# A second token group's linear attention started beside the first, in borrowed tiles, with new due times

## The chip, the cores and the metric

The kernel runs on one core of a Trainium2 chip. The core has five engines with one instruction queue each: TensorE (PE in the profile; its weight loads are PEld) multiplies matrices, VectorE (DVE), ScalarE (ACT) and GpSimd (POOL) work elementwise, and SyncE (SP) here issues every DMA. Each engine executes its own instructions in the order in which they were issued and waits for the other engines by semaphores. The metric is the time of one execution on the device in microseconds (us); lower is better.

## The reference, cut to what matters

The input is 8 sequences of 1024 tokens of width 256, all in float32. Four layers are applied one after the other, each to a layernorm of the running sum `x`:

```python
x = x + _L0_attn_ref(_layernorm(x), ...)   # linear ("flow") attention, then Wo, norm, a 256-1024-256 GELU block, norm
x = x + _L0_ffn_ref(_layernorm(x), ...)    # a 256-1024-256 ReLU block
x = x + _L1_attn_ref(_layernorm(x), ...)   # softmax attention over the whole sequence
x = x + _L1_ffn_ref(_layernorm(x), ...)    # gated block of width 704, inputs and weights rounded to 4-bit values
```

The linear attention of the first layer is where the change is. For one sequence, with `q` and `k` behind a sigmoid:

```python
sink_in = normal / einsum('bhld,bhld->bhl', q + EPS, cumsum(k, axis=2) + EPS)
src_out = normal / einsum('bhld,bhld->bhl', k + EPS, cumsum(q, axis=2) + EPS)
cons_sink = einsum('bhld,bhld->bhl', q + EPS, cumsum(k * src_out[..., None], axis=2) + EPS) / normal
cons_src  = einsum('bhld,bhld->bhl', k + EPS, cumsum(q * sink_in[..., None], axis=2) + EPS) / normal
...
kv = cumsum(einsum('bhld,bhlm->bhldm', k, vs), axis=2)
x  = einsum('bhld,bhldm->bhlm', qs, kv) * sink_alloc[..., None]
```

All the running sums go along the tokens of one sequence, from its first token to its last.

## The kernel before, in words

**Tiles and groups.** Tokens are taken in chunks of 128 (`P`), and chunks in groups of four (`G = 4`, 512 tokens). A sequence has `NCH = 8` chunks and so `NG = 2` groups; the eight sequences have `flows = 16` groups. `divmod(p, NG)` gives the sequence and the half of it that group `p` is: groups 0 and 1 are the first and the second half of the first sequence.

**Stages.** `linear_group(p)` (L998) does the linear attention of one group. Its inner `front(i)` (L1008) takes the chunk `x` that a DMA has loaded, normalizes it, turns it into the columns of `n0T` by `flip` and asks for the chunk four further on. `linear_span` (L1051) then projects `q` and `k` (512 columns a matmul, 256 in group 0, which is cut into two spans), takes the four running sums on VectorE (`running`, L943, which starts from the carry of the group before unless the group opens a sequence), multiplies and sums them by head on TensorE (`head_sums`, L886), and turns the packed results `r1`, `flow`, `e`, `div`, `scale` and `comp` into scales. `spread` (L901) brings packed rows back to full width by way of DRAM, with two `packed` stores and four or two `spread` loads of 256 KB on the SP queue; group 0 does it with small mask matmuls instead (`spread_near`, L922). `linear_chunk` (L1213) does values, scores, the running `kv` and the output projection, chunk by chunk; chunk `c` has its turn when `count["v"] == c`. Its last step hands the normalized `h` over to the dense stage.

`dense` (L1435) runs the two blocks of width 1024. Their weights don't stay: `load_weights` (L1480) streams them again for every group, two buffers of 256 KB for `w_in` and two for `w_out` (`W_FF = 2`). `norms_1` and `norms_2` do what lies between and behind; `norms_2` writes `n2T`, a tile with four buffers, for the softmax layer. `soft_chunk` (L1603) does softmax attention and the 4-bit block for one chunk, and starts for a sequence when both groups of it have passed `norms_2`. Its wide rows lie in three `hid` tiles. `fp4_weights` rounds the weights of the last block once (tiles `w_raw`), `softmax_weights` prepares `wqk` once (tiles `wqk_raw`).

**What sets the order.** No order is written out. All these are generators that a planner, `Plan` (L76), resumes while the program is built. Each `yield` names an engine, the tiles it needs, perhaps a condition (`when`) and a due time (`at`), in units of a group: group `p`'s steps are due at `p` plus a constant from the table `T` (L31). The planner keeps its own clocks of the engines, tiles and DMA rings from costs in `took` (L176). In `run` (L330) it resumes the part with the least key: first how long TensorE would wait, then by how much the part misses a margin of readiness (`RIPE`, from `ripe_t` for TensorE, `ripe_v` for VectorE and so on), then the due time. So every constant of `T` can move instructions anywhere. Two decisions of the planner add work. Where it sees TensorE pause for more than 1.6 us, `fill` (L1757) puts matmuls of the identity with itself there. And `flip` (L683) turns a tile on TensorE when `idle` (L315) finds too little ready for it, or else by a POOL copy (`cut`), a DMA transpose (`spun`) and an ACT copy.

**Order around the change.** `linear_attention` (L1423) runs `linear_group(p)` for `p = 0 ... 15`, one after the other. A group begins when all values of the groups before it are done (`count["v"] == p * G`, L1028), and its projections when the output projections before it are done (`count["linear"] >= p * G`, L1076). It needs `n0T`, `q` and `k`, which have one buffer each (L1029, L1034).

Of the kernel before, what the change touches and what calls it, by code (L numbers as in the profile page):

```python
# [9 lines left out]
F32 = mybir.dt.float32  # L10
# [7 lines left out]
P = 128  # L18
# [6 lines left out]
V_PADS = 2  # L25
HB = P // 2
SCW = P + HB
W_FF = 2
RES = 10
HALVES = 5  # L30
T = dict(  # L31
    span=-0.073, prods=0.117, pair=0.137, sums=0.05, weighted=0.269, sums2=0.303, chunk=0.625,
    scores=0.819, turn_k=0.822, xo=0.419, turn_h=0.629, step=0.095, dense=-0.049, norm=0.528,
    soft=3.5, soft1=0.277, soft2=0.575, soft3=0.75, fp4=3.15, fp4_over=4.022, tail=11,
    weights=0.069, shy=0.745, ripe_t=0.935, ripe_v=0.744, ripe_s=0.298, ripe_g=0.0, ripe_d=6.94,
    back=0.51, ahead=1.173, stage=3, lin=0.0,
)
LAG = 2
QB = 16
G = 4  # L40
GT = G * P
# [34 lines left out]
class Plan:  # L76
# [206 lines left out]
    def pe(self, *tiles, **kw):  # L283
        return self.need("tensor", tiles, **kw)

    def dve(self, *tiles, **kw):
        return self.need("vector", tiles, **kw)
# [4 lines left out]
    def dma(self, *tiles, **kw):  # L292
        return self.need("sync", tiles, **kw)
# [101 lines left out]
def block_stack_kernel(ctx: ExitStack, tc: tile.TileContext, a: dict, out: bass.AP):  # L395
# [20 lines left out]
    plan = Plan(tc, tc.nc)  # L416
    nc, pe, dve, act, dma = plan, plan.pe, plan.dve, plan.act, plan.dma
# [6 lines left out]
    big = ctx.enter_context(tc.tile_pool(name="big", bufs=1))  # L424
# [33 lines left out]
    def kept(shape, name, bufs):  # L458
        t = big.tile(shape, F32, tag=name, name=name, bufs=bufs)
        return t  # L460

    def small(shape, name, bufs=4):
        t = sm.tile(shape, F32, tag=name, name=name, bufs=bufs)
        return t
# [39 lines left out]
    for e in range(2):  # L504
        h = slice(e * HB, (e + 1) * HB)
# [32 lines left out]
    hids = [const.tile([P, INTER_PAD], F32, name=f"hid{i}") for i in range(TILES["hid"][0])]  # L538
# [74 lines left out]
    xs = {c: load_x(c) for c in range(2)}  # L613
# [123 lines left out]
    def two(t):  # L737
        return t.rearrange("p (k t) -> p k t", k=2)
# [144 lines left out]
    weights = set()  # L883
# [59 lines left out]
    def running(out, cur, carry, b, first, last):  # L943
# [14 lines left out]
    flows = B * NG  # L958
    seqs = [{"past": {"chunks": 0}, "n2T": {}, "vt": {}, "normed": 0} for _ in range(B)]
    groups = [  # L960
        {"res": {}, "hT": {}, "nT": {}, "turned": {}, "scaled": set(), "ran": set()}
        for _ in range(flows)
    ]
    count = {
        "halves": 0,
        "dense": 0,
        "acc": 0,
        "res": 0,
        "v": 0,
        "scored": 0,  # L970
        "attended": 0,
        "linear": 0,
# [25 lines left out]
    def linear_group(p):  # L998
        s, g = divmod(p, NG)
        past = seqs[s]["past"]  # L1000
        first, last = g == 0, g == NG - 1
        if first:
            past["cur"] = small([P, 4], "carry_cur", 2)
            past["w"] = small([P, 4], "carry_w", 2)

        n0T = None

        def front(i):  # L1008
            c = p * G + i
            x = xs.pop(c)  # L1010
            yield dve(x, when=lambda: count["res"] < RES)
            count["res"] += 1
            rc = groups[p]["res"][i] = kept([P, D], "res", RES)
            n0 = yield from layernorm("n0", x)
            plan.drop(x)
            yield from flip(two(n0), n0T[:, :, i * P : (i + 1) * P], near=p == 0)
            fronts.add(i)
            yield plan.need("gpsimd", (n0, bo), when=lambda: "norm" in late)
            nc.gpsimd.tensor_tensor(rc, n0, bo, ALU.add)
            plan.drop(n0)  # L1020
            if c + G < B * NCH:
                need = dma(when=lambda: count["stage"] >= 2)
                need.fresh = "x"
                yield need
                xs[c + G] = load_x(c + G)

        fronts = set()
        yield dve(at=p + T["lin"], when=lambda: count["v"] == p * G)  # L1028
        n0T = two(kept([P, 2 * GT], "n0T", 1))  # L1029
        for i in range(G):  # L1030
            plan.start(front(i), p + T["lin"] + 0.5 * T["step"] * i - (p == 0 and i < 2))
        tiles = SimpleNamespace(
            n0T=n0T,
            qk=[kept([P, 2, GT], name, 1) for name in ("q", "k")],  # L1034
            total=small([P, 1], "total", 2),
            ahead=small([P, 1], "ahead", 2),
            comp=small([P, G, 32], "comp", 1),
            packed={n: small([P, P], n, 1) for n in ("r1", "flow", "e", "div", "scale")},
        )
        if first:  # L1040
            past["before"] = None
        else:
            past["before"] = past["total"]
        past["total"] = tiles.total

        spans = (range(0, 2), range(2, 4)) if p == 0 else (range(G),)
        for span in spans[1:]:
            plan.start(linear_span(p, span, fronts, tiles), p + 0.01)
        yield from linear_span(p, spans[0], fronts, tiles)

    def linear_span(p, span, fronts, tiles):  # L1051
# [3 lines left out]
        first, last = g == 0, g == NG - 1  # L1055
        opens, closes = first and span.start == 0, last and span.stop == G
        ran = groups[p]["ran"]
# [3 lines left out]
        r1, flow, e, div, scale = (  # L1061
            tiles.packed[n][rows] for n in ("r1", "flow", "e", "div", "scale")
        )
        n0T, qk = tiles.n0T, tiles.qk
# [2 lines left out]

        def turn(n):

            return lambda: span.start == 0 or (n, span.start) in ran  # L1070


        yield pe(
            at=p + T["lin"] + T["span"] + after,
            when=lambda: fronts >= set(span)
            and count["linear"] >= p * G  # L1076
            and turn("flows")(),
        )
        cur = [qk[b // 2][:, b % 2, here] for b in range(4)]
        for b in (2, 0, 3, 1):  # L1080
# [18 lines left out]
        prods = [None] * 4  # L1099
        for n, pair in enumerate(((2, 0), (3, 1))):  # L1100
            for b in pair:
                need = dve(cur[b], at=p + T["lin"] + T["prods"] + T["pair"] * n + after, when=turn("flow"))
# [15 lines left out]
        if near:  # L1118
            weighted = yield from spread_near(flow, span, ((2, 0), (3, 1)))
        else:  # L1120
            weighted = yield from spread(flow, (2, 0, 3, 1))
        count["stage"] = max(count["stage"], 2)

        for n, pair in enumerate(((2, 0), (3, 1))):
            for b in pair:
                w = weighted[b]
                need = dve(w, at=p + T["lin"] + T["weighted"] + T["pair"] * n + after, when=turn("scale"))
# [40 lines left out]
        ahead = tiles.ahead[rows]  # L1168
# [36 lines left out]
        comp = tiles.comp  # L1205
# [215 lines left out]
        yield from turn_half(p, "hT", i, h)  # L1421

    def linear_attention():  # L1423
        for p in range(flows):
            yield from linear_group(p)
        yield pe(when=lambda: count["linear"] == B * NCH)
        plan.spare = True
        for n in ("q", "k"):
            h = kept([P, 2, GT], n, 1).rearrange("p k t -> p (k t)")
            nc.gpsimd.memset(h[:, INTER:INTER_PAD], 0.0)  # L1430
            hids.append(h[:, :INTER_PAD])
        plan.size["hid"] += 2


    def dense():  # L1435
# [44 lines left out]
        def load_weights(names, used, loaded, first):  # L1480

            ws, n = [], 0
            for p in range(flows):
                for name in names:
                    for f in 2 * list(range(0, NF, 2)):
                        yield dma(
                            at=p + 0.9 + T["weights"] + (2 * n % 32 + (0 if first else LAG)) / 32,
                            when=lambda: n < W_FF + used[0] // 2 and count["stage"] >= 2,
                            unused=ws[n - W_FF :][:1] if n >= W_FF else (),
                        )  # L1490
                        tag = "w_in" if first else "w_out"
                        w = big.tile([P, 2, 2 * P], F32, tag=tag, name=tag, bufs=W_FF)
                        if first:
                            src_ = a[name][:, f * P : (f + 2) * P].rearrange("(k p) n -> p k n", p=P)
                            views = [w[:, :, j * P : (j + 1) * P] for j in range(2)]
                        else:
                            src_ = a[name][f * P : (f + 2) * P, :].rearrange("(j p) n -> p j n", p=P)
                            views = [w[:, j, :] for j in range(2)]
                        nc.sync.dma_start(out=w, in_=src_)
                        ws.append(w)  # L1500
                        loaded.extend(views)
                        n += 1
# [6 lines left out]
        for p in range(flows):  # L1509
            for b, (kind, ba, func) in enumerate((("hT", b1, AF.Gelu), ("nT", fb1, AF.Relu))):  # L1510
                for half in range(2):
# [3 lines left out]
                    for f in range(NF):  # L1515
                        yield pe(
                            at=p + 1 + (16 * b + 8 * half + f) / 32 + T["dense"],
                            when=lambda: n_turned.get((kind, half)) == 2 and w_in and "dense" in late,
                        )
                        inT = groups[p][kind][half]  # L1520
                        w = w_in.pop(0)
# [289 lines left out]
```

## Time and profile before

| | |
|---|---|
| median of 3 runs | 2498.13 us (2496.53 to 2499.07) |
| the profiled execution | 2495.58 us |
| its span, first to last instruction | 2493.9 us |
| busy share: PE, PEld, DVE, ACT, POOL | 98%, 77%, 76%, 56%, 49% |
| instructions in the trace | 47900 |
| mean granted TensorE clock | 0.995 |
| dense matmuls `half,w_in` and `w_out,hidden` (2048 records each) | 530.1 and 528.5 us busy |
| DMA | 311.57 MB, mean 125 GB/s; 759 DMA transposes |

A row of groups reads: line, engine, operation, output and inputs by the program's tile names, shapes, count; then busy time in us and the mean duration of one in ns; then the idle time of the engine just ahead of these instructions, and what ended it. Every instruction of this kernel is issued through one helper, so all stand under L376, and the tile names tell them apart. A float32 matmul of the program appears as two records, a transpose as one. Durations on TensorE overlap[...].

### The profile page before, as it was taken

What the parts mean: (1) busy time and instruction counts of PE and PEld (TensorE: products, weight loads), DVE (VectorE), ACT (ScalarE), POOL (GpSimd) and SP (SyncE); (2) the same over time, 40 slices, a digit from 0 to 9 for tenths busy, and PEclk for the clock granted to TensorE, in tenths of its full rate; (3) what the DMA queues carried; (4) which work ended last, traced back from release to release, by engine and by line L of the source; (5) the groups of instructions that cost most, each with busy time, mean ns of one, the idle gap of its engine ahead of it and who ended that gap; (6) DMA issues with size and microseconds to landing.
All of it is one profiled execution on the core that took longest, in us unless ns stands there. A gap on an engine that the chain in (4) does not pass through costs nothing.

```text
span 2493.9 us, 47900 instructions
## 1 busy us (share of the span) xinstructions
PE 2445.0 (98%) x16609; PEld 1910.6 (77%) x16609; DVE 1901.3 (76%) x4151; ACT 1392.5 (56%) x2903; POOL 1228.8 (49%) x2249
## 2 busy tenths in 40 slices
PE   8999899999999999999999999999999999999998
PEld 7777777777777877777787777778777787877667
DVE  7677667777869778696877868787786978866877
ACT  4535456555565656555555665655656555555454
POOL 3324446464554646545474555636455564644342
PEclk9999999999999999999999999999999999999999
DMA  3244455555555555556555555546555565545342
GB/s 92 66 137 128 128 140 143 132 128 129 134 130 131 132 138 123 137 122 149 130 134 136 127 133 140 136 116 146 132 133 124 129 141 131 133 117 132 66 83 57
DMA packets 626002, 311.57 MB, mean 125 GB/s; under 512 B 429408, under 2 KB 614240, under 8 KB 625760
## 3 DMA queue, kind: packets, MB, share of 16 engines
q1 hardware_dynamic: 625760, 308.52, 50.8%
q8 instruction: 131, 2.15, 0.4%
q14 instruction: 111, 0.91, 0.1%
HBM read 188.17 MB, written 20.71 MB: 84 GB/s over the span
## 4 chain that ended last, share of the span: by engine, by line
PE 80%; DVE 4%; POOL 1%; issue 1%; ACT 0%; DMA 0%; DVEq 0%; POOLq 0%; ACTq 0%
PE bank L376 80%; DVE hid L376 1%; DVE x_amax L376 0%; DVE k L376 0%; POOL cut L376 0%; DVE n L376 0%; POOL ln_rstd L376 0%; DVE q L376 0%; DVE x_r L376 0%; DVE ln_st L376 0%; DVE mx L376 0%; DVE x_s L376 0%; DMA spun<-cut 0%; DVE u L376 0%; DVE y L376 0%
## 5 line engine op out<-in xcount | busy, mean ns | idle before, releaser
L376 PE MATMUL bank<-w_out,hidden 128*128 128x256 f32 x2048 | 528.5, 385 | 10.1 <-DMA w_out<-in_L_attn_W_dram 6.3
L376 PE MATMUL bank<-half,w_in 128*128 128x256 f32 x2048 | 530.1, 382 | 4.1 <-ACT half L376 4.1
L376 PEld LDWEIGHTS bank<-w_out,hidden 128*128 128x128 f32 x2048 | 379.0, 191 | 120.3 <-issue 58.8
L376 PEld LDWEIGHTS bank<-half,w_in 128*128 128x128 f32 x2048 | 386.2, 191 | 80.2 <-issue 18.8
L376 POOL TENSOR_SCALAR ln_ve<-ln_mv 128x1 f32<-128x1 f32 x384 | 105.1, 274 | 599.4 <-DVE ln_mv L376 580.1
L376 ACT ACTIVATE hidden<-bank,c_L_ffn_b 128x256 f32<-128x256 f32 x256 | 121.1, 474 | 259.8 <-PE bank L376 258.9
L376 POOL TENSOR_TENSOR ln_rstd<-ln_ve,neghalf 128x1 f32<-128x1 f32 x384 | 235.1, 612 | 32.0 <-POOL ln_ve L376 0.2
L376 PE MATMUL bank<-n2T,qT 128*128 128x512 f32 x512 | 241.1, 594 | 2.3 <-ACT qT L376 2.3
L376 ACT ACTIVATE hidden<-bank,c_L_attn_b 128x256 f32<-128x256 f32 x256 | 120.0, 470 | 208.4 <-PE bank L376 206.8
L376 PE MATMUL bank<-vt,probT 128*128 128x256 f32 x1024 | 231.6, 379 | 0.0
L376 PEld LDWEIGHTS bank<-vt,probT 128*128 128x128 f32 x1024 | 194.1, 190 | 29.3 <-issue 2.2
L376 POOL COPY cut<-n 128x512 uint16<-128x512 uint16 x223 | 152.3, 692 | 120.3 <-DVE n L376 63.4
L376 POOL COPY cut<-hid 128x512 uint16<-128x512 uint16 x168 | 125.3, 773 | 132.2 <-DVE hid L376 124.8
L376 ACT COPY probT<-spun 128x512 uint16<-128x512 uint16 x246 | 159.2, 672 | 33.3 <-DMA spun<-cut 33.2
L376 PE MATMUL bank<-wdT,hqT 128*128 128x256 f32 x768 | 177.2, 380 | 0.0
L376 PE MATMUL bank<-wgT,xqT 128*128 128x352 f32 x512 | 173.3, 461 | 0.7 <-ACT xqT L376 0.5
L376 PE MATMUL bank<-wuT,xqT 128*128 128x352 f32 x512 | 172.3, 459 | 0.0
L376 POOL COPY cut<-prob 128x512 uint16<-128x512 uint16 x209 | 142.6, 706 | 55.7 <-ACT prob L376 36.1
L376 ACT ACT_TABLE_LOAD x128 | 164.2, 1283 | 8.6 <-PE bank L376 6.4
L376 PEld LDWEIGHTS bank<-wdT,hqT 128*128 128x128 f32 x768 | 144.5, 190 | 22.4 <-issue 1.3
L376 PEld LDWEIGHTS bank<-n2T,qT 128*128 128x128 f32 x512 | 96.5, 190 | 72.2 <-issue 60.5
L376 PEld LDWEIGHTS bank<-wuT,xqT 128*128 128x128 f32 x512 | 97.3, 190 | 54.2
(243 smaller groups left out, 4833.3 us busy)
## 6 DMA issues: line engine op xcount, KB each, us to landing
w_in<-in_L_attn_W_dram SPq DMA_DIRECT2D x128, 256.0 KB
w_out<-in_L_attn_W_dram SPq DMA_DIRECT2D x128, 256.0 KB
w_in<-in_L_ffn_w_dram SPq DMA_DIRECT2D x128, 256.0 KB
w_out<-in_L_ffn_w_dram SPq DMA_DIRECT2D x128, 256.0 KB
spread<-packed SPq DMA_DIRECT2D x90, 256.0 KB
spun<-cut SPq DMA_TRANSPOSE x759
x<-in_L_attn_inputs_dram SPq DMA_DIRECT2D x64, 128.0 KB
xr<-in_L_attn_inputs_dram SPq DMA_DIRECT2D x64, 128.0 KB
```

The source lines that it names most:

```text
L376: ins = method(*args, **kw)
```

## The change

The first two groups are started together, and group 1 works in other tiles. `linear_attention` starts `linear_group(0)` as a part of its own and runs the others in sequence from group 1 on. Group 1 (`aside`) may begin as soon as its four `x` chunks are loaded, and its projections don't wait for group 0's outputs; its first running sums wait until group 0's last span has passed the mark `("flow", G)`, its weighted ones for the mark `("scale", G)`. Its `n0T`, `q` and `k` are three of the four `n2T` buffers, and its six packed tiles are thirds of the second and third `hid` tile. Group 2 now waits for group 0's values alone before it begins (`done = G`). Group 0's `x` chunks ask for those of group 1 one stage earlier. Nine constants of `T` get new values: `prods`, `sums2`, `turn_h`, `step`, `dense`, `fp4`, `weights`, `ripe_t` and `back`. `W_FF` is split into `W_IN` and `W_OUT`, which are 2 both.

```diff
-W_FF = 2
+W_IN, W_OUT = 2, 2
...
-    span=-0.073, prods=0.117, pair=0.137, sums=0.05, weighted=0.269, sums2=0.303, chunk=0.625,
-    scores=0.819, turn_k=0.822, xo=0.419, turn_h=0.629, step=0.095, dense=-0.049, norm=0.528,
-    soft=3.5, soft1=0.277, soft2=0.575, soft3=0.75, fp4=3.15, fp4_over=4.022, tail=11,
-    weights=0.069, shy=0.745, ripe_t=0.935, ripe_v=0.744, ripe_s=0.298, ripe_g=0.0, ripe_d=6.94,
-    back=0.51, ahead=1.173, stage=3, lin=0.0,
+    span=-0.073, prods=0.129, pair=0.137, sums=0.05, weighted=0.269, sums2=0.231, chunk=0.625,
+    scores=0.819, turn_k=0.822, xo=0.419, turn_h=0.635, step=0.092, dense=-0.115, norm=0.528,
+    soft=3.5, soft1=0.277, soft2=0.575, soft3=0.75, fp4=2.285, fp4_over=4.022, tail=11,
+    weights=0.209, shy=0.745, ripe_t=1.247, ripe_v=0.744, ripe_s=0.298, ripe_g=0.0, ripe_d=6.94,
+    back=0.511, ahead=1.173, stage=3, lin=0.0,
...
-                need = dma(when=lambda: count["stage"] >= 2)
+                need = dma(when=lambda: count["stage"] >= (2 if p else 1))
...
-        yield dve(at=p + T["lin"], when=lambda: count["v"] == p * G)
-        n0T = two(kept([P, 2 * GT], "n0T", 1))
+        aside = p == 1
+        done = {0: 0, 1: 0, 2: G}.get(p, p * G)
+        yield dve(
+            at=p + T["lin"],
+            when=lambda: count["v"] >= done and all(p * G + i in xs for i in range(G)),
+        )
+        n0T = two(kept([P, 2 * GT], "n2T" if aside else "n0T", 4 if aside else 1))
...
-            qk=[kept([P, 2, GT], name, 1) for name in ("q", "k")],
+            qk=[two(kept([P, 2 * GT], "n2T", 4)) if aside else kept([P, 2, GT], name, 1) for name in ("q", "k")],
...
+        names = "r1", "flow", "e", "div", "scale", "comp"
+        if aside:
+            parts = [h[:, j * P : (j + 1) * P] for h in hids[1:] for j in range(3)]
+        else:
+            parts = [small([P, P], n, 1) for n in names]
+        tiles.packed = dict(zip(names, parts))
+        tiles.comp = tiles.packed["comp"].rearrange("p (t r) -> p t r", t=G)
...
-            return lambda: span.start == 0 or (n, span.start) in ran
+            if span.start:
+                return lambda: (n, span.start) in ran
+            if p == 1:
+                return lambda: (n, G) in groups[0]["ran"]
+            return lambda: True
+
+        done = {1: 0, 2: G}.get(p, p * G)
...
-            and count["linear"] >= p * G
-            and turn("flows")(),
+            and count["linear"] >= done
+            and (span.start == 0 or turn("flows")()),
...
-        for p in range(flows):
+        plan.start(linear_group(0), 0.0)
+        for p in range(1, flows):
             yield from linear_group(p)
...
+            bufs = W_IN if first else W_OUT
...
-                            when=lambda: n < W_FF + used[0] // 2 and count["stage"] >= 2,
-                            unused=ws[n - W_FF :][:1] if n >= W_FF else (),
+                            when=lambda: n < bufs + used[0] // 2 and count["stage"] >= 2,
+                            unused=ws[n - bufs :][:1] if n >= bufs else (),
```

More of the change, by code (lines that the diff above doesn't have):

```diff
@@ L1033, in linear_group @@
             n0T=n0T,
-            qk=[kept([P, 2, GT], name, 1) for name in ("q", "k")],
+            qk=[two(kept([P, 2 * GT], "n2T", 4)) if aside else kept([P, 2, GT], name, 1) for name in ("q", "k")],
             total=small([P, 1], "total", 2),
             ahead=small([P, 1], "ahead", 2),
-            comp=small([P, G, 32], "comp", 1),
-            packed={n: small([P, P], n, 1) for n in ("r1", "flow", "e", "div", "scale")},
-        )
+        )
+        names = "r1", "flow", "e", "div", "scale", "comp"
[5 more added lines that the diff above has]
+        tiles.comp = tiles.packed["comp"].rearrange("p (t r) -> p t r", t=G)
         if first:
@@ L1487, in load_weights @@
                             at=p + 0.9 + T["weights"] + (2 * n % 32 + (0 if first else LAG)) / 32,
-                            when=lambda: n < W_FF + used[0] // 2 and count["stage"] >= 2,
-                            unused=ws[n - W_FF :][:1] if n >= W_FF else (),
+                            when=lambda: n < bufs + used[0] // 2 and count["stage"] >= 2,
+                            unused=ws[n - bufs :][:1] if n >= bufs else (),
                         )
                         tag = "w_in" if first else "w_out"
-                        w = big.tile([P, 2, 2 * P], F32, tag=tag, name=tag, bufs=W_FF)
+                        w = big.tile([P, 2, 2 * P], F32, tag=tag, name=tag, bufs=bufs)
                         if first:
```

## The prediction

> **What bounds the kernel now.** I read the engine totals of the page first, then the chain that ended last, then the busy time by stretch, and last the order of TensorE in the stretches that stand out.
>
> ```profile
> PE 2445.0 (98%) x16609; PEld 1910.6 (77%) x16609; DVE 1901.3 (76%) x4151; ACT 1392.5 (56%) x2903; POOL 1228.8 (49%) x2249
> ...
> PE 80%; DVE 4%; POOL 1%; issue 1%; ACT 0%; DMA 0%; DVEq 0%; POOLq 0%; ACTq 0%
> ```
>
> TensorE is busy 98% of the span and holds 80% of the chain. So time can come only from TensorE: from what it executes, from its 48.9 us of idleness (2493.9 - 2445.0), or from its clock. Whether what it executes is all work is in the groups (count, busy, mean, idle before):
>
> ```profile
> L376 PE MATMUL bank<-ident 128*128 128x128 f32 x400 | 50.7, 287 | 3.1 <-POOL ident masks.py:199 3.1
> L376 PE MATMUL bank<-ident,n 128*128 128x128 f32 x66 | 11.8, 276 | 3.6 <-DVE n L376 2.7 <-ACT n L376 0.8
> ```
>
> The first row is no work: identity times identity, which `fill` (L1757) puts where the planner expects TensorE to pause over 1.6 us. A matmul of the program is two records here, so these are 200. The second is transposes on TensorE, one record each. By stretch (columns: busy us and instructions of PE, PEld, DVE, ACT, POOL, then granted clock, DMA share, GB/s):
>
> ```profile
> 0.00:60.00 60.00, 50.27 (x513) 43.96 (x513) 42.22 (x112) 25.73 (x71) 18.29 (x50) 1.00 0.33 96
> 60.00:130.00 70.00, 63.80 (x522) 50.74 (x522) 48.08 (x116) 34.84 (x89) 22.23 (x47) 0.93 0.23 68
> 130.00:400.00 270.00, 250.11 (x2015) 200.80 (x2016) 195.02 (x438) 137.30 (x305) 120.81 (x234) 0.97 0.49 135
> 400.00:2450.00 2050.00, 2043.84 (x13376) 1585.98 (x13376) 1584.38 (x3430) 1179.67 (x2411) 1058.96 (x1907) 1.00 0.54 128
> 2450.00:2494.00 44.00, 36.95 (x186) 29.13 (x184) 31.66 (x57) 15.01 (x29) 8.54 (x13) 1.00 0.23 51
> ```
>
> Of the idleness 9.7, 6.2 and 19.9 us lie in the first 60, the next 70 and the next 270 us, 6.2 in the long middle, 7.1 at the end. The opening also has the low clock. The rows of TensorE's timeline there (start, length, then idle before) show what those losses look like:
>
> ```profile
> 61.38 1.91 PE L376 MATMUL bank<-half,w_in 128*128 128x256 f32 x4
> 63.08 0.63 PE L376 MATMUL bank<-ident,wqk_raw 128*128 128x128 f32 x2
> ...
> 84.69 8.65 PE L376 MATMUL bank<-ident 128*128 128x128 f32 x76
> 93.17 0.38 PE L376 MATMUL bank<-ident,n 128*128 128x128 f32 x2
> ...
> 142.77 1.87 PE L376 MATMUL bank<-w_out,hidden 128*128 128x256 f32 x4 [3.52 <-DMA w_out<-in_L_ffn_w_dram]
> ...
> 250.93 3.75 PE L376 MATMUL bank<-w_out,hidden 128*128 128x256 f32 x8 [4.70 <-DMA w_out<-in_L_attn_W_dram]
> ```
>
> Durations overlap, so I cost by start to start. 38 fills take 93.17 - 84.69 = 8.48 us, 0.223 each: 200 are 44.7 us. The half-weight row at 61.38 takes 1.70 us to the next start, against 0.86 for the same row at 77.26: half clock. The ten-us slices at 60, 100, 110, 140, 160, 240 and 250 us grant 0.83, 0.77, 0.89, 0.83, 0.83, 0.94, 0.72: 11.9 us lost. The ledger of losses is 44.7 + 48.9 + 11.9 = 105.5 us, and the opening 400 us hold most of it.
>
> **What changes, by the order of the two built programs.** Group 1 of the planner is tokens 512 to 1023 of the *same* sequence (two groups per sequence), so its running sums still take group 0's carry. Only its norms and projections are free of that.
>
> *Fills* (counted in the order): ahead of the first dense matmul 86 become 74; from there to the first projection of group 2, 73 become 39; up to the end region 12 become 7; in the end 29 become 35. Net 200 to 155: -45 x 0.223 = **-10.1 us**.
>
> *Work moved forward:* the eight 512-column matmuls of group 1 go ahead of the first dense one. In the trace two of them take 114.80 - 113.08 = 1.72 us, so 6.9, plus four transposes at 0.11 (93.17 to the next two): 7.3 us. It adds nothing; it stands where fills and waits stood.
>
> *Transposes:* 17 fewer on TensorE, x 0.11 = **-1.9 us**. Eight DMA transposes and about eight cut copies more (0.69 us each on POOL, 5.5 us) lie under engines at 49% busy; if that cover were gone they would cost 5.5.
>
> *Tile switches:* changes between 32-wide and 128-wide matmuls go from 286 to 296. Two groups in the steady middle repeat every 294.7 us, where their matmuls at start-to-start rates sum to 290.7; less 0.8 idle that is 3.2 us over about 36 switches, 0.09 each: **+0.9**.
>
> *Idleness and new waits.* No trace shows the new order, so I bound each stretch.
> - To the first dense matmul (60.03 us before). On VectorE four statistics (0.41 + 0.18 each) and a 1.4 us scan of group 1 now stand ahead of group 0's `h` rows, with three passes on raw weights (1.3) gone: a slip of 0 to 2.5 us for everything behind, and TensorE waits for `h`. The matmul sum to there goes from 44.0 to 48.7. Before, 60.0 - 44.0 = 16.0 was 9.7 idle and 6.3 of starts and switches; with the full slip, 62.5 - 48.7 - 6.3 leaves 7.5 idle, without it 5.0. I take 7.5 (-2.2), as VectorE has no slack until its 5.6 us wait at 44.
> - To 130 us: fills of 13, 9 and 12 stand close together, where one of 38 stood with 5.8 us of idleness round it. 5 to 11, I take 8 (+1.8).
> - To 400 us: 8.2 of the 19.9 are the two waits for `w_out` above. At 242.45 and 135.53 us the SP queue issues four 256 KB `spread` loads for 2.5 us, and the weights behind them come late. The new order has such a set too, so I keep 8.2. The other 11.7 go with the fills of this stretch, 47 to 12: 3.0. Sum 11.2 (-8.7); bounds 6 and 20.
> - Middle 6.2 to 7, end 7.1 to 8 (six more fills there): +1.7; bounds 0 and +6.
> Sum **-7.4 us**.
>
> A cross-check on VectorE: to group 1's last scale it has 104 us of work at the rows' durations. At the 78% that it kept in the old order up to the same step (129 of 165 us), that comes at 134 us. The old kernel had finished 78 us of real matmul work by then, the new order has 80 before that point. So the gain is small there and comes mostly after it, where groups 1 and 2 no longer starve TensorE.
>
> *Clock.* Here a rule of the Trainium skill stands against the row. "TensorE: Matmul & The Clock Gate", section "HAM oscillation", says the clock halves for gaps over some 3.4 us. By it only the gaps of 3.52 and 4.70 would cost, both of which stay, and the clock term is 0; and taking fills out of pauses below that length is free. The trace disagrees: the half rate at 61.38 us follows a stretch whose largest gap is 1.04 us (2.7 idle in ten), that at 106 follows 1.63 and 2.00. I take the trace: seven windows of 1.7 us, of which two go with the fills after 130 us: **-3.4**, bounds +3 and -7.
>
> *Borrowed tiles.* Three of four `n2T` buffers and two `hid` are group 1's until its last chunk. The first sequence's second `n2T` and the softmax chunks want them later, when their own inputs come out of the dense stage of group 1; I cost it at nothing, and if that cover is gone it is one wait of a chunk, about 2 us.
>
> *SP queue.* Two transposes of group 1 now stand ahead of four `x` loads and the raw weights; SP waits there for POOL's cuts. The raw softmax weights were issued by 24.7 us and used at 61, so 30 us of cover; without it each us of delay would cost one.
>
> Sum: -10.1 - 1.9 + 0.9 - 7.4 - 3.4 = -21.9. The profiled execution took 2495.6 (span 2493.9): 2473.7 there, a span of 2472.0. The median of the runs shown lies 2.5 above it: **2476 us**, -0.9%. What a measurement can tell from no change is 0.2%, 5 us.
>
> **Rivals.**
> 1. *The head only trades fills for waits.* Group 1's sums need group 0's carry, VectorE runs at 78 to 83%, and what was fill becomes idle at the same places. For it: the cross-check, and the 2.0 us waits for raw weights at 106 us. Against: the matmul sum before the dense stage does grow by real work. Idle +10, clock 0: 2498.1 - 10.1 - 1.9 + 0.9 + 10 = 2497. This is also the case that the change does not do what it says, since nothing but projections can run beside group 0. Chance 0.12.
> 2. *Slower: weights behind spreads in the middle.* The due time of weight loads moves from 0.069 to 0.209, and in the new order they stand round the `spread` sets in ever other ways instead of one repeated pattern. A wait as at 250.93 costs 4.7 plus a window of 1.7: 6.4 us. Four would use up the gain, five make it slower; six give 2476 + 38 = 2514. Against it: from 400 us on, the thirteen groups with spreads left 6.2 us idle in all, and the readiness margin of TensorE's parts is raised (0.935 to 1.247). Chance 0.11.
> 3. *More gain:* the waits for `w_out` also go (8.2) and all seven clock windows (another 8.5): 2459. Chance 0.07.
>
> **Numbers.** My forecast has 0.70, with 2464 to 2492 as its own range. Faster by over 0.2%: 0.70 + 0.07 = 0.77; within it 0.12; slower 0.11. The range of 8 in 10 runs from 2462, half of the deep case left out, to 2500, which takes in the first rival; outside are most of the second and half of the third.
>
> **What would show it.** A fill row of 310 records instead of 400, TensorE busy 2425 to 2435, idleness up to 400 us of about 27 instead of 36, the granted clock low in five slices rather than seven, and 400 to 2450 us still above 99.5% busy. I am wrong if the middle shows new idleness on `w_out` or `w_in`, or if idleness between 60 and 150 us rises by as much as the fills fall.

## The result, and the profile after

The changed kernel takes **2475.64 us** (median of 4 runs, 2473.4 to 2477.65) against 2498.6 us for the kernel before, measured beside it (4 runs, 2496.53 to 2500.68). The ratio is 0.9908, with a 95% interval of 0.9891 to 0.9925: faster by 0.9%. The forecast was 2476. The profiled execution took 2475.61 us, its span 2473.9 us, 20.0 less than before (the medians differ by 23.0).

The page of the changed kernel, totals of the engines and then the chain that ended last:

```profile
PE 2431.3 (98%) x16503; PEld 1896.0 (77%) x16503; DVE 1893.8 (77%) x4139; ACT 1397.6 (56%) x2913; POOL 1233.7 (50%) x2257
...
PE 88%; DVE 7%; DMA 2%; ACT 1%; POOL 1%; issue 1%; SPq 0%; DVEq 0%; ACTq 0%; POOLq 0%
```

TensorE still bounds the kernel. It is busy for 13.7 us less and idle for 6.3 us less (42.6 against 48.9), which makes up the 20.0. The group of fills accounts for most of the busy time that went:

```profile
L376 PE MATMUL bank<-ident 128*128 128x128 f32 x310 | 39.6, 288 | 3.1 <-POOL ident masks.py:199 3.1
```

That is 90 records fewer and 11.1 us less (50.7 before). The other 2.6 us lie in the rest of the busy time; there are some 16 transposes fewer and fewer slices at a low clock, and what each gave was not separated. The busy time by stretch (columns as before the change):

```profile
0.00:60.00 60.00, 51.39 (x417) 39.71 (x421) 40.29 (x106) 31.21 (x79) 23.40 (x59) 0.94 0.38 106
60.00:130.00 70.00, 63.06 (x633) 53.91 (x626) 58.70 (x131) 31.58 (x84) 23.61 (x44) 0.98 0.26 75
130.00:400.00 270.00, 256.35 (x2087) 205.66 (x2086) 198.09 (x467) 143.22 (x326) 137.22 (x263) 0.99 0.55 143
400.00:2450.00 2050.00, 2042.28 (x13270) 1582.05 (x13269) 1583.64 (x3417) 1184.75 (x2414) 1045.44 (x1885) 1.00 0.53 127
2450.00:2474.00 24.00, 18.20 (x108) 14.63 (x106) 13.06 (x21) 6.79 (x12) 4.05 (x6) 0.98 0.26 56
```

Subtract each busy time from its stretch: TensorE is idle for 8.6, 6.9, 13.7, 7.7 and 5.8 us. The first 130 us have 15.5 us of it, as against 15.9 before; the real fall, 6.2 us, is from 130 to 400 us.

A fill is time without work just as idleness is, so I add the two. From here on **pauses** means the span less TensorE's busy time, plus the busy time of the fills, for each stretch of a profile:

| kernel | to 130 us | 130 to 400 | after 400 | sum | median of the runs, us |
|---|---|---|---|---|---|
| before | 46.5 | 31.4 | 21.6 | 99.5 | 2498.6 |
| changed | 43.8 | 16.8 | 21.7 | 82.3 | 2475.64 |

17.2 of the 20 us are pauses, and 14.6 of these lie between 130 and 400 us. What is left of the span beside the pauses is not the same in every kernel: it is 2394.4 and 2391.6 us here, and 2388 to 2399 us in the runs below that have fills. So pauses show where time was won, and the runs' medians how much. The waits of TensorE in that stretch, before (us in total, times, longest):

```profile
PE bank L376 <- DMA w_out<-in_L_attn_W_dram: 6.3, 2, 4.7
PE bank L376 <- DMA w_out<-in_L_ffn_w_dram: 3.5, 1, 3.5
PE bank L376 <- ACT half L376: 2.6, 3, 1.3
PE bank L376 <- ACT k L376: 2.2, 1, 2.2
PE bank L376 <- ACT e L376: 2.1, 1, 2.1
```

and in the changed kernel:

```profile
PE bank L376 <- ACT half L376: 7.2, 4, 2.8
PE bank L376 <- DMA w_out<-in_L_attn_W_dram: 1.9, 1, 1.9
PE bank L376 <- DMA w_in<-in_L_attn_W_dram: 1.8, 1, 1.8
```

The waits for `k` and `e` are gone (the one for `e` is group 1's own, see experiment 3); those for weights fell from 9.8 to 3.7 us; the waits for the normalized input `half` of the dense stage grew by 4.6.

### The profile page after: what moved, and what is told of

Read it like the earlier page. It is cut to its first block, busy times and chain, and to the rows that moved or that the text cites. A ratio compares the mean times of both kernels' runs of the same rounds, so it can differ in the third digit from the quotient of the medians.

```text
span 2473.9 us, 47678 instructions
## 1 busy us (share of the span) xinstructions
PE 2431.3 (98%) x16503; PEld 1896.0 (77%) x16503; DVE 1893.8 (77%) x4139; ACT 1397.6 (56%) x2913; POOL 1233.7 (50%) x2257
## 3 DMA queue, kind: packets, MB, share of 16 engines
q8 instruction: 131, 2.15, 0.4%
## 4 chain that ended last, share of the span: by engine, by line
PE 88%; DVE 7%; DMA 2%; ACT 1%; POOL 1%; issue 1%; SPq 0%; DVEq 0%; ACTq 0%; POOLq 0%
PE bank L376 88%; DMA spun<-cut 1%; DVE hid L376 1%; DVE prod L376 1%; DVE u L376 0%; DVE n L376 0%; DVE ln_st L376 0%; DVE x_amax L376 0%; POOL ln_rstd L376 0%; DVE w_raw L376 0%; DVE res L376 0%; POOL cut L376 0%; DVE div L376 0%; POOL ln_shift L376 0%; DVE ln_mv L376 0%
## 5 line engine op out<-in xcount | busy, mean ns | idle before, releaser
L376 POOL COPY cut<-n 128x512 uint16<-128x512 uint16 x238 | 170.9, 726 | 96.7 <-DVE n L376 58.0
L376 POOL COPY cut<-hid 128x512 uint16<-128x512 uint16 x165 | 117.6, 736 | 154.3 <-DVE hid L376 133.9
L376 ACT ACT_TABLE_LOAD x128 | 164.2, 1283 | 3.7 <-PE bank L376 1.5
```

The lines of the kernel that those rows point to most:

```text
L376: ins = method(*args, **kw)
```

## The experiments

**Theory A, as I began:** the gain comes from the structure (tiles of their own for group 1, early conditions), which keeps later groups from starving TensorE after 130 us, and new due times are only needed to use it. **Rivals:** the due times alone do it; the fills that left were the gain; or the gain is made in the head, by running two groups beside each other. The first six runs were taken against the kernel before at 2499.96 (e1 to e4) and 2499.23 us (e5, e6), the next four at 2499.36, the last two at 2498.5. In all but e3 and e4 the planner orders the whole program anew, so such a run shows its edit together with the order that follows from it.

### 1. Structure alone, due times alone

The new structure with the old table (`T` row by row as before the change; one row of it):

```diff
-    weights=0.209, shy=0.745, ripe_t=1.247, ripe_v=0.744, ripe_s=0.298, ripe_g=0.0, ripe_d=6.94,
+    weights=0.069, shy=0.745, ripe_t=0.935, ripe_v=0.744, ripe_s=0.298, ripe_g=0.0, ripe_d=6.94,
```

> The new structure (group 1 beside group 0) with the nine old due times. Theory A, the ledger (time moves by what TensorE executes plus idleness plus clock): its order has 196 fills (4 fewer than before, -0.9 us), 181 transposes (10 fewer, -1.1), 282 tile switches (-0.4); fills behind the first dense matmul are 93 where the changed kernel has 46, so little of the idleness goes: 2490 to 2498 us. Rival: the structure alone carries the gain and the due times are noise: 2476 to 2480 us.

Measured: 2483.78 us (ratio 0.9934, 0.9919 to 0.9948). Between the two expectations, and against my sum: there are 392 fill records, 8 fewer than before, and yet 16 us are gone. Pauses are 43.4, 21.7 and 26.5 us: 3.1 and 9.7 less than before up to 400 us, 4.9 more after it. So the structure carries some two thirds of the gain, and the pauses that it takes away lie mostly from 130 to 400 us. The due times then take away 4.9 us more there and 4.8 after 400 us.

The old structure with the new table (one row of it):

```diff
-    weights=0.069, shy=0.745, ripe_t=0.935, ripe_v=0.744, ripe_s=0.298, ripe_g=0.0, ripe_d=6.94,
+    weights=0.209, shy=0.745, ripe_t=1.247, ripe_v=0.744, ripe_s=0.298, ripe_g=0.0, ripe_d=6.94,
```

> The old structure with the nine new due times. Theory A: 240 fills (40 more than before, +8.9 us), 185 transposes (-0.7), 292 switches (+0.5), idleness up with the fills by some 5: 2505 to 2515 us. Rival: the due times alone carry the gain: 2476 to 2482 us.

Measured: 2502.52 us (ratio 1.0011, 1.0004 to 1.0018), with 480 fill records and pauses of 41.1, 40.5 and 23.3 us. The due times by themselves gain nothing; the rival that they do it falls. The waits for `w_out` from 130 to 400 us tell the same: 9.8 us are left with the new due times alone, and none among the larger waits with the structure alone.

### 2. Are the fills a cost?

In both kernels the identity matmuls are left out of the program, while the planner still books them, so that the order of all else is the same. What is left out computes nothing that is used.

```diff
-            nc.tensor.matmul(bank[:, :P], lhsT=ident, rhs=ident, start=True, stop=True)
+            plan.took("tensor", "matmul", (bank[:, :P],), dict(lhsT=ident, rhs=ident))
```

> The kernel before with the identity matmuls left out (they compute nothing that is used); the planner still books them, so that the rest of the order stays. Theory A: a fill stands in a wait that something else ends, so the wait remains: matmul busy time falls by about 45 us, idleness rises by about 40, and the clock falls in more windows of 1.7 us each: 2500 to 2515 us. Rival: fills cost what they last, and fewer fills are themselves the gain: 2455 to 2465 us.

> The changed kernel with the identity matmuls left out in the same way, the order else the same. Theory A: 2478 to 2490 us, idleness up by about 31 us, some windows more at half clock. Rival (fills cost what they last): 2441 to 2450 us. The difference to the kernel before without fills should stay near 20 us by A, since what went with the fills is the waits under them; it should shrink to 10 us by the rival.

Measured: 2499.99 us for the kernel before without fills (ratio 1.0002, 0.9994 to 1.0011) and 2485.07 us for the changed one without (0.9941, 0.9924 to 0.9958). The opening of the kernel before without its fills:

```profile
0.00:60.00 60.00, 36.28 (x337) 26.76 (x337) 38.85 (x106) 24.76 (x67) 16.83 (x47) 0.86 0.32 95
60.00:130.00 70.00, 55.45 (x416) 41.68 (x417) 50.99 (x122) 35.37 (x92) 23.30 (x49) 0.85 0.22 64
130.00:400.00 270.00, 241.68 (x1961) 191.82 (x1960) 195.82 (x437) 136.42 (x303) 119.10 (x232) 0.96 0.53 135
```

The idle time to 400 us is now 66.6 us where it was 35.8, and the granted clock is 0.86 and 0.85 where it was 1.00 and 0.93. Added up over whole ten-us slices, the clock falls short by 28.8 us up to 400 us, against 11.9 before; TensorE is idle in part of these slices, so its work lost less than that. Over the whole span, the fills' 50.7 us of busy time came back as 36.9 us of idleness (85.8 against 48.9) and 17.8 us by which the busy time of all other matmuls grew (2394.3 to 2412.1). The low clock is part of these 17.8 us; how large a part was not separated. Together it is 4.0 us more, as the two profiled spans say, and nothing in the medians. **Fills are not a cost by themselves; they lie in pauses that other engines make**, and in the changed kernel they are worth 8 to 9 us. Between the two kernels without fills the difference is still 14.9 us, halfway between the 20 that I expected and the 10 of the rival, and idleness falls by 16.2 us (85.8 to 69.6): the change takes pauses away, whether these are filled or not.

### 3. Beside, or early?

The structure has two conditions. In the first experiment group 1 begins only when group 0's values are done, as before; its own tiles and the early group 2 stay:

```diff
-        done = {0: 0, 1: 0, 2: G}.get(p, p * G)
+        done = {0: 0, 2: G}.get(p, p * G)
```

> The changed kernel, but group 1 begins when the values of group 0 are done, as before the change; it still has tiles of its own, group 2 still begins early, and all due times are the new ones. Theory 1 (the gain of the structure lies after 130 us, because later groups have tiles of their own and can start when TensorE would otherwise wait; running beside group 0 in the head itself earns nothing): 2474 to 2482 us, idleness from 130 to 400 us about as in the changed kernel, 12 to 17 us. Theory 2 (group 1 must be under way in the head for its work to be past when the dense blocks begin): 2488 to 2498 us, with 17 us or more of idleness from 130 to 400 us. On the slip of the head: if the projections of group 1 are what held group 0 up on TensorE, the first transpose of `scale` is back at 36 to 38 us and the first dense matmul at 60 to 62 us; if they stay near 44 and 69 us, the cause lies elsewhere.

In the second, group 1 stays beside group 0, and group 2 has its old conditions, in both places:

```diff
-        done = {0: 0, 1: 0, 2: G}.get(p, p * G)
+        done = {1: 0}.get(p, p * G)
...
-        done = {1: 0, 2: G}.get(p, p * G)
+        done = {1: 0}.get(p, p * G)
```

> The changed kernel, but group 2 begins only when all values of group 1 are done and all its linear outputs are counted, as before the change; group 1 runs beside group 0. Theory 1 (what pays is that every later group may start early): group 2's first projections come some rows later on TensorE, 2479 to 2487 us, with idleness from 130 to 400 us up by 3 to 8 us. Theory 2 (what pays is group 1 in the head, and group 2's condition is not what starts it): 2474 to 2478 us. The first dense matmul stays at 69 us by both.

Measured: not beside, 2486.81 us (0.9952, 0.9937 to 0.9967); group 2 late, 2483.79 us (0.994, 0.9923 to 0.9957).

| kernel | to 130 us | 130 to 400 | after 400 | sum | median, us |
|---|---|---|---|---|---|
| changed | 43.8 | 16.8 | 21.7 | 82.3 | 2475.64 |
| e7, not beside | 42.2 | 27.4 | 21.2 | 90.8 | 2486.81 |
| e8, group 2 late | 42.6 | 22.5 | 20.5 | 85.6 | 2483.79 |

Both conditions pay, 11 and 8 us, and **both pay from 130 to 400 us**. The rows of e7 (two stretches, and its group of fills):

```profile
0.00:130.00 130.00, 116.41 (x1036) 97.11 (x1037) 91.82 (x234) 62.64 (x167) 39.84 (x96) 0.99 0.32 91
130.00:400.00 270.00, 256.88 (x2129) 208.24 (x2128) 204.73 (x452) 137.59 (x309) 128.08 (x242) 0.99 0.51 137
...
L376 PE MATMUL bank<-ident 128*128 128x128 f32 x394 | 51.2, 292 | 3.1 <-POOL ident masks.py:199 3.1
```

From 130 to 400 us TensorE is as busy as in the changed kernel (256.88 and 256.35 us), but 14.3 us of it are fills, against 3.1. Up to 130 us the head without the second group has no more pauses than with it.

Where these pauses stand is seen at one step of group 1, its `total,front` and the transpose of its `scale` on TensorE. Before the change:

```profile
159.62 0.38 PE L376 MATMUL bank<-total,front 128*128 128x1 f32 x2 [2.11 <-ACT e L376]
...
160.17 6.71 PE L376 MATMUL bank<-ident 128*128 128x128 f32 x44
166.71 0.27 PE L376 MATMUL bank<-ident,scale 128*128 128x128 f32 x1
```

in e7, where group 1's `e` and `scale` lie in `hid` tiles:

```profile
152.08 0.38 PE L376 MATMUL bank<-total,front 128*128 128x1 f32 x2 [2.11 <-ACT hid L376]
...
152.55 6.79 PE L376 MATMUL bank<-ident 128*128 128x128 f32 x44
159.17 0.27 PE L376 MATMUL bank<-ident,hid 128*128 128x128 f32 x1
```

and in the changed kernel:

```profile
121.26 0.28 PE L376 MATMUL bank<-total,front 128*128 128x1 f32 x2
...
121.62 1.11 PE L376 MATMUL bank<-half,w_in 128*128 128x256 f32 x4
...
126.02 0.27 PE L376 MATMUL bank<-ident,hid 128*128 128x128 f32 x1
```

In the first two, TensorE waits 2.11 us for `e` and then runs fills while VectorE makes `scale` of it: 8.7 us of pause in each (the fills outlast this work by 2.5 us). In the changed kernel the same step comes 38 and 31 us earlier, without a wait, and matmuls of group 0's dense stage stand where the fills stood. This one place is 8.7 of the 10.6 us of pauses that e7 has more in this stretch. In e8 the waits for the dense weights stand out instead: 8.8 us of this stretch, against 3.7 in the changed kernel; why they come later there was not traced. Both runs keep the changed kernel's due times, and whether other due times would win a part back was not tried.

So Theory A was half right: the gain does lie after 130 us, but running beside is needed for about half of it. (My first theory of e7 said 2474 to 2482, the second 2488 to 2498; the measurement is just below the second. The idleness from 130 to 400 us, 13.1 us, is as the first said; what differs is fills.) Running beside moves group 1's chain to where group 0's dense matmuls cover it.

### 4. The late first dense matmul

The forecast let group 0's chain slip by 2.5 us; the first dense matmul came at 69.23 us instead of 60.03. TensorE's timeline of the changed kernel (start, length, idle before):

```profile
35.00 0.27 PE L376 MATMUL bank<-total,front 64*64 64x1 f32 x2 [1.29 <-ACT e L376]
36.50 0.69 PE L376 MATMUL bank<-ident,n 128*128 128x128 f32 x2 [1.23 <-ACT ahead L376]
37.65 3.78 PE L376 MATMUL bank<-n2T,wk 128*128 128x512 f32 x4 [0.46 <-ACT n2T L376]
41.22 2.63 PE L376 MATMUL bank<-n2T,wq 128*128 128x512 f32 x4
43.79 0.28 PE L376 MATMUL bank<-ident,scale 64*128 64x64 f32 x1
...
69.23 1.13 PE L376 MATMUL bank<-half,w_in 128*128 128x256 f32 x4 [0.46 <-ACT half L376]
```

VectorE has `scale` ready at 39.69 us, but group 1's projections stand before its transpose in TensorE's queue, and at half clock: the first pair takes 3.57 us from start to start, where 1.72 were measured before the change. I took that for the cause of the slip, and first held these projections until `scale` was issued on VectorE:

```diff
-            and (span.start == 0 or turn("flows")()),
+            and (span.start == 0 or turn("flows")())
+            and (p != 1 or ("scale", 2) in groups[0]["ran"]),
```

> The changed kernel with group 1's projections held until the packed scale of group 0's first half is done, so that they no longer stand ahead of its transpose on TensorE (where it lay ready for 4.1 us). Theory A: the first dense matmul comes at 64 to 66 us instead of 69.2; but the re-planned order has 191 fills (36 more, +8.0 us) and 201 transposes (26 more, +2.9), so the whole is 2478 to 2488 us. Rival: the start of the dense stage sets the end, and every us there is one at the end: 2466 to 2472 us.

Measured: 2491.49 us (0.996, 0.9946 to 0.9974); the transpose moved only to 41.85, the first dense matmul to 68.68. Later than the expected 64 to 66 us and above the 2478 to 2488, but inconclusive: issued on VectorE is not done, and one of the pairs still stood ahead on TensorE. The rest of the order was planned anew and had 382 fill records. So I set the mark behind the transpose itself:

```diff
         nc.tensor.transpose(bank, scale, ident[rows, rows])
+        ran.add(("turned", span.stop))
...
+            and (p != 1 or ("turned", 2) in groups[0]["ran"]),
...
-    weights=0.209, shy=0.745, ripe_t=1.247, ripe_v=0.744, ripe_s=0.298, ripe_g=0.0, ripe_d=6.94,
+    weights=0.209, shy=0.745, ripe_t=1.2, ripe_v=0.744, ripe_s=0.298, ripe_g=0.0, ripe_d=6.94,
```

> The changed kernel, but group 1's projections may be issued only after group 0's first transpose of scale; group 1 still runs beside group 0 (ripe_t is 1.2 instead of 1.247, without which the planner finds no order; 0.935 was measured at no more than 2 us). Theory (the projections in front of it on TensorE are what delays group 0, and the delay is paid for by the work done meanwhile): the transpose of scale starts at 37 to 39 us instead of 43.8, the first dense matmul at 62 to 66 us instead of 69.2, and idleness plus fills up to 130 us stay within 3 us of the changed kernel's 44; the whole 2478 to 2490 us, since the rest is planned anew with 79 more fill instructions. Rival (the slip of the head is itself a loss): idleness plus fills up to 130 us fall to 39 or less.

Measured: 2491.57 us (0.9974, 0.9963 to 0.9986), just above the expectation. Its TensorE timeline:

```profile
36.78 4.71 PE L376 MATMUL bank<-ident 128*128 128x128 f32 x22
41.43 0.28 PE L376 MATMUL bank<-ident,scale 64*128 64x64 f32 x1
...
44.42 1.88 PE L376 MATMUL bank<-n2T,wk 128*128 128x512 f32 x4
...
56.90 1.88 PE L376 MATMUL bank<-n2T,wk 128*128 128x512 f32 x4
...
68.08 1.13 PE L376 MATMUL bank<-half,w_in 128*128 128x256 f32 x4
```

and the transpose and the first dense matmul in e7, where group 1 does not run beside:

```profile
37.86 0.24 PE L376 MATMUL bank<-ident,scale 64*128 64x64 f32 x1
...
61.37 1.13 PE L376 MATMUL bank<-half,w_in 128*128 128x256 f32 x4 [0.46 <-ACT half L376]
```

Counted from the first projection of group 0, which starts at 11.47, 12.51, 12.82 and 11.77 us:

| | `scale` done | then its transpose starts | then first dense matmul | sum |
|---|---|---|---|---|
| before | 24.90 | 0.15 | 23.51 | 48.56 |
| changed | 27.18 | 4.10 | 25.44 | 56.72 |
| e7, not beside | 24.89 | 0.15 | 23.51 | 48.55 |
| e11, transpose first | 27.71 | 1.95 | 26.65 | 56.31 |

e7 returns to the old head to a hundredth: group 1 beside is the whole slip, 8.2 us. But the theory that its projections in front of one transpose are the whole cause **falls**: with them behind it, 2.15 of the 4.10 us of waiting go, and 0.5 and 1.2 us come back on either side (before `scale`, and behind the transpose, where the projections now stand). The 1.95 us that stay are no longer projections: 22 fill records stand there, at half rate too (0.21 us each from start to start, 0.11 in the fills before the change). I expected 62 to 66 us and got 68.08. The slip is shared out over the whole chain of group 0: 2.3 us up to `scale`, 3.9 at the transpose, 1.9 after it in the changed kernel. Up to 130 us the slip is not itself a loss: pauses there are 46.1 in e11, 43.8 in the changed kernel, 42.2 in e7 and 46.5 before, whether the dense stage begins at 60 or at 69 us. Whether it costs anything later, no run separates. e11 loses behind 130 us, with 19.7 us of fills after 400 us (8.3 in the changed kernel), as the rest was planned anew.

### 5. Is it the carry?

Group 1 is the second half of the same sequence, so its running sums wait for group 0's carry. Here group 1 is the first half of the second sequence, with no carry to wait for; group 2 is the second half of the first. (The running `kv` of that sequence lies in the unused `hid` tile.)

```diff
+    def place(p):
+        return {1: (1, 0), 2: (0, 1)}.get(p, divmod(p, NG))
...
-        s, g = divmod(p, NG)
+        s, g = place(p)
```

> The second planner group is truly another sequence: the first half of sequence 1 takes the place of the second half of sequence 0, which becomes the third group, so nothing of it waits for group 0's carry. Theory A: the first sequence's softmax starts a group later and work is missing at the end; the order has 219 fills (64 more than the changed kernel, 56 of all in the end region, +14 us) and 213 transposes (+4): 2490 to 2505 us, though idleness between 60 and 150 us falls. Rival: the carry is what holds the head back, and freeing it gains 5 to 10 us: 2466 to 2471 us.

Measured: 2516.76 us (1.0062, 1.0047 to 1.0077), slower than before the change and above both expectations. The first dense matmul comes at 69.23 us again: the carry is not what holds the head up. Pauses are 46.6, 32.0 and 38.2 us. The first sequence is complete one group later and the end of the kernel is worse; which wait makes the 38.2 was not separated.

### 6. Which due time?

The changed kernel with one entry of the old table each. First `fp4=3.15` and `ripe_t=0.935`:

> The changed kernel with one due time set back: fp4 3.15 as before instead of 2.285. On TensorE its order has the same fills as the changed kernel. If this number carries the last 8 us between the new structure with old due times and the changed kernel: 2481 to 2485 us. If it carries none: 2474 to 2477 us. I expect the second, at even odds with something between.

> The changed kernel with one due time set back: ripe_t 0.935 as before instead of 1.247 (when transposes count as ripe). Its order has 34 more fills, most of them after 400 us. If what is ripe late keeps spare work for TensorE's gaps in the middle, and this number carries the last 8 us: 2480 to 2486 us, idleness plus fills from 400 to 2450 us up by 5 us or more. If not: 2474 to 2478 us.

Measured: 2476.62 us (0.9908, 0.9894 to 0.9923) and 2477.57 us (0.9915, 0.9901 to 0.993). Neither differs from the changed kernel by what can be told, although e10 has 68 fill records more and its pauses from 400 to 2450 us are 17.5 us where the changed kernel has 9.2, a larger rise than the 5 us that I had set as the sign of a loss. Then `weights=0.069`, by which the dense weights are due to be loaded earlier:

> The changed kernel with one due time set back: weights 0.069 as before instead of 0.209, so that the loads of the dense weights are listed earlier. Its order has the head of the changed kernel row by row, but 239 fill instructions instead of 155, most of the extra ones after 400 us. If fills as the planner counts them are time lost: 84 fills at 0.22 to 0.26 us each, 2492 to 2498 us. If the waits on w_out that the earlier loads take away pay for it: 2470 to 2480 us. By the switch from the old set of due times as a whole (8 us): 2481 to 2486 us.

Measured: 2492.4 us (0.9976, 0.9965 to 0.9986), as the first expectation said. The group of fills:

```profile
L376 PE MATMUL bank<-ident 128*128 128x128 f32 x478 | 60.5, 285 | 3.1 <-POOL ident masks.py:199 3.1
```

Its pauses are 44.7, 16.4 and 43.0 us: the head and the stretch to 400 us are the changed kernel's, and what it is slower lies after 400 us, where 238 fill records (28.9 us) stand against 70 (8.3 us); what they wait for was not traced. With *all* old due times the loss is 8 us (e1), with this one alone 17: the entries act as a set, not as a sum. Three of the nine were tried.

## Why the prediction was right, and where it was not

- **The sum.** Span: -21.9 foreseen, -20.0 measured. Fills -10.1 (45 x 0.223 is 10.0), measured -11.1, from exactly the 310 records that the order had shown; the 11.1 is busy time, in which a fill counts somewhat longer than from start to start. Idleness -7.4, measured -6.3. Transposes and switches -1.0 and clock -3.4, measured together -2.6 (busy time without fills: 2394.3 to 2391.7). TensorE's busy time (2431.3), the middle stretch at 99.6% and the low clock in five slices up to 400 us (6.8 us lost there, 11.9 before) fell as said; a sixth slice, at 610 us, gave 1.7 back. That there are five such slices is partly luck: only the one at 110 us is among the seven of before, and up to 130 us the shortfall is 5.1 us in both kernels. What went is after 130 us (6.8 to 1.7).
- **By stretch.** Idleness to 130 us 15.5 foreseen (7.5 + 8), 15.5 measured; 130 to 400 us 11.2, measured 13.7 (so 29.2 up to 400 us, not about 27); middle 7 and 7.7; end 8 and 5.8. That the gain "is small there and comes mostly after it" held: 2.7 of 17.2 us of pauses before 130 us. The cross-check put group 1's last `scale` at 134 us; it was ready at 124.7, under group 0's dense matmuls, and 164.2 before.
- **The mis-sized term: the slip of group 0.** "A slip of 0 to 2.5 us for everything behind", from VectorE alone; measured 8.2, plus 1.0 by which the whole head began later. Up to `scale` it is 2.3, within what I had given to VectorE. Left out were TensorE's own queue and rate: a wait of 4.1 us at one transpose, behind two projection pairs that took 6.1 us where 3.4 are two at the rate before the change. That the total still held is no merit of this step: meanwhile TensorE did work that it would have had to do later, and the pauses up to 130 us did not grow (e7, e11).
- **A wrong reading that did no harm: what the fills are.** I priced each fill at 0.223 us and took it for a saving. For e12 that price would do: 84 more of them, 16.8 us, 0.20 each. For e10 it doesn't: 34 more, 1.9 us. They are a gauge, and a rough one, not the cause: with none at all the kernel before takes the same time (e3), and e1 gains 16 us with nearly all of them left. Pauses are the better term. e1 went wrong for me by just this: I had scaled its idleness with its fills.
- **The waits for `w_out`.** I kept 8.2 us of them, because four `spread` loads still stand ahead of weights; 1.9 are left, and 1.8 on `w_in`. They go with the structure (e1 against e2); by which step was not traced. The waits for `half` that I did not foresee took 4.6 of it back, so idleness in this stretch came out 2.5 us above my sum instead of below it.
- **Rivals.** The first (the head trades fills for waits) was right that the head gains little, but no trade took place: up to 130 us fills went from 30.6 to 28.2 us and idleness from 15.9 to 15.5, and the gain behind it came. The second (weights behind spreads in the middle) did not come: there is no wait on weights among the larger ones after 400 us. e12 shows the price of the other direction of that due time. The third was 17 us too deep.
- **The rule on gaps.** Again the trace did not keep to the limit of about 3.4 us that the Trainium skill gives ("TensorE: Matmul & The Clock Gate", section "HAM oscillation"). Ten-us slices of the changed kernel:

```profile
30.00:40.00 10.00, 5.37 (x29) 2.81 (x29) 8.42 (x18) 4.82 (x15) 3.62 (x5) 0.80 0.18 52
40.00:50.00 10.00, 10.00 (x46) 5.48 (x45) 4.63 (x13) 4.25 (x12) 1.58 (x4) 0.86 0.51 148
```

No gap in the first of them is over 1.29 us, yet from 30 us to the pair at 37.65 us TensorE is busy for 3.0 of 7.65 us (the rows stand in experiment 4), and that pair runs at half rate. So pauses well below that length went with a low clock here. How low the busy share must be for it is not shown: the first ten us of the changed kernel, busy for 6.90, read 1.00. That the fills of the changed kernel are worth 8 to 9 us (e4) fits this.

## What to carry to other kernels

Count pauses (idleness plus filler work) by stretch; fillers alone show neither what was gained nor why. Starting independent work early pays where TensorE would later have waited for it, even if the head gets no better and its first result comes later: ask which later wait the moved work takes away, and which other work then covers it. And when a planner sets the order, test due times as a set: single entries gave 1, 2 and 17 us in the structure where the whole set gave 8.

## What the runs showed of the hardware that was not expected

- Filler matmuls earn their keep only partly. In the kernel before, leaving out 50.7 us of them gave 36.9 us of idleness and 17.8 us of longer work, and the time stayed the same to 0.1%; in the changed kernel leaving out 39.6 us gave 27.0 and 21.6 us, and cost 8 to 9 us.
- A low clock can fall on a chain that others wait for. Behind 7.65 us with no gap over 1.29 us but only 3.0 us of work, two projection pairs took 6.1 us instead of 3.4, ahead of group 0's `scale` in TensorE's queue; in e11 it was fills that ran there at half rate. Long gaps went with it too: without fills (e3) the slice from 30 to 40 us, with a gap of 3.53 us and one of 3.01, read 0.50.
